# A four-layer image kernel: exponentials of one block on another engine, and statistics and copies in other places

## The chip, the cores and the metric

The kernel runs on one core of a Trainium2 chip. A core has engines that run side by side, each with its own queue of instructions: TensorE (PE in the profile; its weight loads are listed as PEld), which multiplies matrices into the accumulator memory PSUM; VectorE (DVE), which works elementwise; ScalarE (ACT), which evaluates functions such as the exponential; GpSimd (POOL); and SyncE (SP), which here only issues transfers (DMA) to and from the memory outside the core. Working data lies in the on-chip memory SBUF, 128 partitions wide. The metric is the device time of one execution in microseconds (us); less is better.

## The reference

The input `x` has shape (2, 128, 64, 64): two images of 128 channels, fp32. Four layers follow one another, each of the form `x = x + L(gn(x))`, where `gn` is a group normalization with 32 groups of four channels:

```python
def _gn(v, G=32, eps=1e-5):
    ...
    m = jnp.mean(g, axis=(2, 3, 4), keepdims=True)
    s = jnp.var(g, axis=(2, 3, 4), keepdims=True)
    return ((g - m) / jnp.sqrt(s + eps)).reshape(v.shape)
```

Layer 0 is an attention of four heads with convolutions around it; the change does not touch it. Layer 1 is a mix of convolutions; the two that matter here are `t8 = _conv(x, w8, (4, 4), dilation=(2, 2), groups=c)`, a 5 x 5 filter on each channel alone (25 "taps"), and a product with a matrix for each of seven rows. Layer 2 multiplies in the frequency domain: `rfft2` of the image, a product with complex 32 x 32 matrices at each of 64 x 33 frequencies, combined as quaternions, and `irfft2`. Layer 3 is a softmax attention with eight heads of 16 channels over all 4096 positions:

```python
a = jnp.einsum('bhcq,bhck->bhqk', q, k) / jnp.sqrt(jnp.float32(C))
a = jax.nn.softmax(a, axis=-1)
o = jnp.einsum('bhqk,bhck->bhcq', a, v)
```

## The kernel before, in words

**Frame.** The image stays in SBUF as `X`, 128 channels by 2 images by 4096 positions; each layer adds its output onto `X`. A chunk is 512 positions (`CH`), eight to an image. The layers run one after the other: layer 0 until 1500 us of the profile, layer 1's main part from 1537 to 1795, layer 2 to 2117, layer 3 to 3990. Within a layer the helper `_in_order` keeps TensorE's, VectorE's, ScalarE's and GpSimd's instructions in the order in which the program writes them; nothing is reordered. Side work is written as Python generators, and where a `next(...)` (or `some(gen, n)`, n times `next`) stands in the main loop decides where its instructions stand in each queue. Transfers are issued by SyncE in the order in which the program and their data allow.

**Statistics.** `_stats_steps` (L1433) computes a group normalization's mean and 1/sigma of one image in eleven steps. Each of the first eight measures one chunk on VectorE (L1444); the ninth combines them (L1447); the tenth has one TensorE matmul that averages over a group (L1450), followed by three small VectorE operations; the eleventh has a second such matmul (L1462), and then a VectorE operation (L1429) and a power on GpSimd (L1430). A normalization is `scale * x + shift`, so a shift, minus the mean times the scale, is needed as well.

**Layer 1, main part.** For each image, eight chunks follow one another. For each, TensorE runs `combined` (L710, the rows' products, 14 matmul records in the profile) and, before chunks 0 and 2, `on_tiles` (L681, the first four taps as diagonal matrices; ScalarE copies them out, L691). VectorE then adds the previous chunk's result onto `X` (`added`, L721), and `some(rest, ...)` (L760) advances the second image's remaining taps, 2 to 4 VectorE operations of 2.4 us each (L662). After them `some(steps, 2)` (L761) takes two steps of the statistics of image 0, which layer 2 will use; the steps exist only while image 1 runs.

**Layer 2.** First `shifted` (L851) makes the shift of image 0 on VectorE; `normalized` (L860) makes the normalized image on ScalarE (L868), `columns` (L882) transposes it on TensorE with a VectorE copy (L888), and `transformed` does the first Fourier step. Then eight blocks `kb` of frequency rows follow. In each, `products` (L1002) multiplies the spectrum by the layer's weights in two runs, the "direct" rows and the "mirrored" rows; weights arrive by DMA. Beside a run of products, `alongside` advances a list of generators: `rows_in` (L983) transposes and transforms rows of the spectrum on TensorE and then copies them (`placed`, L946) into the operand `e`, permuted and signed as the quaternion product wants it. A row needs twelve copies, of which eight, those with `r` 1 and 3, are of 32 partitions by 136 elements. In each pair of rows the first row's copies go to ScalarE (L960) and the second's to VectorE (L962). Block 0 has no previous block's output to work on, so beside its direct products the side list (L1128) holds the copies for its own mirrored products: those of the first pair of rows, and transposition, transformation and copies of the second pair. At the layer's end each image is turned back in eight steps: `turned_back` (L1154) transposes on TensorE, ScalarE copies, `added` (L1169) transforms and VectorE adds onto `X`; the two are skewed by `_skewed`, so that one is a step ahead of the other. While image 1 is turned back, each step takes two steps (L1163) of image 0's statistics for layer 3.

**Layer 3.** The heads and images form four groups (image `b`, half `t`), each with eight query blocks of 512 positions, and for each block 32 key tiles of 128 positions. For each tile, `scores` (L2311) fills two accumulators of two banks each (L2316, four matmuls of the program); for each of the two, the exponential is taken by ScalarE in one operation (L2330, 128 x 1024) or, for the pairs in `BY_VECTOR` (L1332), by VectorE with a polynomial: `exponentials` (L2269) makes eight VectorE operations (L2272, L2277, L2280, four of L2288, L2292), advanced one step a tile. There are four such pairs a block, at tiles 5, 12, 20 and 27. Three tiles (`LAG`) after the scores `multiply` (L2332) adds the product of the exponentials with the values onto the block's accumulator (L2339); the tables `ORDER` (L1344) put the pairs computed by VectorE some six tiles, for the last one four tiles, later in that sum. Three score accumulators take six PSUM banks. The two banks left (`acc`) serve the block's running product, the projections of queries, keys and values, and the bound.

The first block of the first group is also where that group's operands are made. `queries_and_keys` (L2190) makes, for one chunk, a projection (L2197), two shuffles (L2200, L2202) and five more elementwise operations (on ScalarE for the first two chunks, otherwise VectorE: L2211 to L2216), sends the three results out by DMA (L2219, `stack`), and reduces their largest absolute values (L2223). `stacked` (L2233) brings them back in the layout that the scores need, query pieces `q` and key pieces `k`. `values` (L2238) makes the values of four tiles (L2243, and one VectorE addition, L2250). These generators are advanced by one step every second tile until they are done; after that the bound (`bound`, L2257: VectorE L2260 and L2262, a matmul L2264, VectorE L2266) is taken. The later groups' operands are made during the group before.

**Other names.** The tile `st` (L2536) holds means and scales for layers 0 to 3. Layer 1 gets a view `there` of it, in which it leaves the statistics of image 0 for layer 2, which gets the same view as `here`.

Of the kernel before, what the change touches and what calls it, by code (L numbers as in the profile page):

```python
# [10 lines left out]
F32 = mybir.dt.float32  # L11
AF = mybir.ActivationFunctionType
ALU = mybir.AluOpType
# [6 lines left out]
NCH = S // CH  # L20
# [511 lines left out]
def _layer1(ctx, tc, X, a, cst, here=None, there=None, consts=None):  # L532
# [190 lines left out]
    def some(gen, n):  # L723
        for _ in range(n):
            next(gen, None)
# [23 lines left out]
    for b in range(B):  # L749
        for c in range(NCH):  # L750
            if c in (0, 2):
                z = on_tiles(g[b], t2[b], c // 2)
            ps = combined(t9[b], t2[b], c)

            for x in ready:
                added(*x)
            ready = [(b, c * CH, ps)]
            if c in (1, 3):
                ready.append((b, c // 2 * S // 2, z))
            some(rest, (4, 2, 4, 2, 3, 2, 2, 2)[c])  # L760
            some(steps, 2)  # L761
        if there is not None and b == 0:
            for x in ready:
                added(*x)
            ready = []
            steps = _stats_steps(nc, two, bank, X[:, 0, :], cst, mhalf, there)
# [36 lines left out]
def _layer2(ctx, tc, X, weights, cst, src, here=None, there=None, beside=None):  # L803
# [26 lines left out]
    with tc.tile_pool(name="l2_a", reuse_waits="tile", bufs=3) as ap, tc.tile_pool(  # L830
# [23 lines left out]
        scales = [st]  # L854
        shifts = [shifted(st)]
        if B > 1:
# [53 lines left out]
    with tc.tile_pool(name="l2_e", reuse_waits="tile", bufs=4) as ep, tc.tile_pool(  # L910
# [34 lines left out]

        def placed(kb, m, got, image, e, scalar):  # L946

# [19 lines left out]
            copied(2, 1)  # L967
            yield
            for r in (1, 3):
                for p in range(4):  # L970
                    copied(r, p)
                yield
# [9 lines left out]

        def rows_in(kb, rows, places, es):  # L983

            yts = [transposed(m) for m in rows]
            yield
            gots = [transformed(m, yt) for m, yt in zip(rows, yts)]
            yield
            yield from copies(kb, rows, gots, places, es)

        def copies(kb, rows, gots, places, es):
            for image in places:
                if es[image] is None:
                    es[image] = ep.tile([128, 4, 2 * PAIRS, 8 * B], F32, tag="e", name="e")
                yield from together(
                    *(
                        placed(kb, m, got, image, es[image], i % 2 == 0)
                        for i, (m, got) in enumerate(zip(rows, gots))
                    )
                )  # L1000
# [114 lines left out]
        for kb in range(BLOCKS2):  # L1115
# [7 lines left out]
            if before:  # L1123
                side += [turned(pzs[1], before[1]), back(kb - 1, *before)]
                n += 6
            else:
                later = side
                side, n = [copies(0, first[:2], gots[:2], (1,), e), rows_in(0, first[2:], (1,), e)], 8  # L1128
            alongside(
# [18 lines left out]
    with tc.tile_pool(name="l2_c", reuse_waits="tile", bufs=3) as cp, tc.tile_pool(  # L1148
        name="l2_cps", reuse_waits="tile", bufs=4, space=PSUM
    ) as cps:  # L1150
        for b in range(B):
            xi = X[:, b, :].rearrange("p (h w) -> p h w", w=W)

            def turned_back(i):  # L1154
                pt = cps.tile([128, CH], F32, tag="pt", name="ps_pt")
                for n in range(4):
# [5 lines left out]
                    )  # L1162
                for _ in range(2):  # L1163
                    next(steps, None)
# [974 lines left out]
def _layer3(ctx, tc, X, l3, cst, out, worst, here, dram):  # L2139
# [158 lines left out]
    class Group:  # L2298

        def __init__(self, b, t, f, idle=0):  # L2300
            self.b, self.t, self.f, self.ac = b, t, f, None
            self.kept, self.q, self.k = {}, {}, {}
            self.vt = two.tile([128, NQT, 2, 3, 16], F32, tag="vt", name="vt")
# [7 lines left out]
    def scores(g, qb, kt):  # L2311
# [11 lines left out]
        for p in range(2):  # L2323
            g.weights[qb, kt, p] = w = []
            if (kt, p) in BY_VECTOR:
                chain[0] = exponentials(ps[p], w)
# [5 lines left out]
    def multiply(g, qb, at):  # L2332
        if at == 0:
            g.ac = acc()
        for j in range(4):

            i, kt = j % 2, ORDER[j // 2][at]
            (w,) = g.weights[qb, kt, j // 2]
# [188 lines left out]
def kernel(ctx, tc, a, out):  # L2527
# [4 lines left out]
    with tc.tile_pool(name="keep", bufs=1) as keep:  # L2532
        X, cst, eps5 = _inputs(tc, keep, a)

        worst = keep.tile([128, 1 + 2 * B], F32, name="worst")
        st = keep.tile([128, B + 2, 2], F32, name="st")  # L2536
        rows_of_weights = _layer0(tc, X, a, cst, worst, st[:, :B], dram)
# [86 lines left out]
```

## Time and profile before

| | |
|---|---|
| time, median of three runs | 4001.92 us (4000.72 to 4008.1) |
| profiled execution, its own time | 4003.18 us |
| its span, first to last instruction | 4001.4 us |
| TensorE busy | 3853.4 us (96%) |
| ScalarE busy | 3243.5 us (81%) |
| VectorE busy | 3200.6 us (80%) |
| GpSimd busy | 86.2 us (2%) |
| DMA | 217.59 MB, mean 54 GB/s |
| mean granted TensorE clock | 0.987 of full speed |

The page gives the busy time of each engine, the same by slices of the span, the chain of work that ended last, and groups of instructions with the idle time before them and what ended it. Shares of the whole span are averages over stages with different limits. By stage, the windows view gives (us):

| stage | length | PE | DVE | ACT |
|---|---|---|---|---|
| layer 1, main part, 1537 to 1795 | 258 | 244.09 | 237.79 | 72.39 |
| layer 2, 1795 to 2117 | 322 | 284.10 | 218.44 | 187.90 |
| layer 3, 2117 to 3990 | 1873 | 1857.37 | 1407.24 | 1785.63 |

Two groups of the page are those of layer 3's exponentials: L2330 on ScalarE, 1920 operations of 1062 ns, busy 1781.3 us; and on VectorE 128 sets of steps, for instance L2272, 128 operations of 1224 ns.

### The profile page before, as it was taken

The numbers are of one execution on the slowest core, as the hardware profiler recorded it, in microseconds if no ns is written. First come the engines' busy times: TensorE is split into PE (matmuls) and PEld (weight loads), VectorE is DVE, ScalarE is ACT, GpSimd is POOL, SyncE is SP. The second block draws the span as 40 slices with busy tenths as digits, with TensorE's granted clock in tenths as the row PEclk, the third lists the DMA queues.
The fourth block names the chain that finished last, engine by engine and source line by source line (L and its number), as shares of the span: only waits on it lengthen the run. The fifth ranks groups of instructions, "written<-read, shape, count | busy, mean of one in ns | idle before, by whom it ended". The sixth has DMA issues, their size and how long they took to land.

```text
span 4001.4 us, 82144 instructions
## 1 busy us (share of the span) xinstructions
PE 3853.4 (96%) x35202; PEld 1313.9 (33%) x35202; DVE 3200.6 (80%) x3577; ACT 3243.5 (81%) x3948; POOL 86.2 (2%) x145
## 2 busy tenths in 40 slices
PE   7999999989999998998998999999999999999998
PEld 4511221353111124446664232232233222322222
DVE  6599999858999998996758777777777777776666
ACT  4499999736899983226645999999999999999998
POOL 1000000000000001000000000000000000000000
PEclk9999999999999999999998999999999999999999
DMA  1199960000000000004744110110002000110000
GB/s 51 23 200 185 187 106 2 1 2 2 2 2 2 2 2 13 6 19 199 280 199 150 32 32 25 53 46 31 26 27 72 30 27 25 44 47 6 6 6 5
DMA packets 193128, 217.59 MB, mean 54 GB/s; under 512 B 30441, under 2 KB 154345, under 8 KB 188658
## 3 DMA queue, kind: packets, MB, share of 16 engines
q1 hardware_dynamic: 192754, 212.25, 20.5%
q8 instruction: 278, 4.55, 0.5%
q14 instruction: 96, 0.79, 0.1%
HBM read 178.64 MB, written 98.57 MB: 69 GB/s over the span
## 4 chain that ended last, share of the span: by engine, by line
PE 78%; DVE 10%; issue 4%; ACT 2%; POOL 0%; SPq 0%; DMA 0%; ACTq 0%; POOLq 0%; DVEq 0%
PE ps_acc L2339 25%; PE ps_s L2316 19%; PE ps L1884 11%; PE ps L1892 11%; DVE X L662 3%; PE ps_z L1024 2%; PE ps_bank L710 2%; DVE sums L1915 2%; PE ps L1645 2%; DVE e L962 1%; PE ps_bank L681 1%; PE ps_bank L1078 1%; PE ps_acc L2197 1%; PE ps_acc L2243 1%; PE ps_pe L937 1%
## 5 line engine op out<-in xcount | busy, mean ns | idle before, releaser
L2330 ACT ACTIVATE weights<-ps_s 128x1024 f32<-128x1024 f32 x1920 | 1781.3, 1062 | 75.6 <-PE ps_s L2316 75.4
L2339 PE MATMUL ps_acc<-weights,vt 128*32 128x512 f32 x8192 | 1092.9, 605 | 0.0
L1915 DVE TENSOR_TENSOR sums<-sums,weights 128x2048 f32<-128x2048 f32 x384 | 854.2, 2283 | 3.5 <-ACT weights L1967 1.4
L2316 PE MATMUL ps_s<-q,k 64*128 64x512 f32 x4096 | 830.3, 469 | 3.7 <-DMA k<-stack 2.4
L1967 ACT ACTIVATE weights<-ps 128x1536 f32<-128x1536 f32 x512 | 740.6, 1447 | 6.9 <-PE ps L1892 6.9
L2316 PEld LDWEIGHTS ps_s<-q,k 64*128 64x128 f32 x4096 | 348.3, 184 | 935.2 <-ACT weights L2330 808.8
L1892 PE MATMUL ps<-q,k 32*64 32x512 f32 x8192 | 574.0, 612 | 3.6 <-ACT weights L1964 3.0
L1884 PE MATMUL ps<-weights,vt 128*32 128x512 f32 x4096 | 544.7, 604 | 0.0
L2288 DVE SCALAR_TENSOR_TENSOR exp_z<-exp_z,exp_m 128x1024 f32<-128x1024 f32 x384 | 469.0, 1221 | 9.3
L1964 ACT ACTIVATE weights<-ps 128x512 f32<-128x512 f32 x512 | 306.8, 599 | 75.3 <-PE ps L1892 36.5
L2272 DVE TENSOR_SCALAR exp_i<-ps_s 128x1024 int32<-128x1024 f32 x128 | 156.7, 1224 | 216.7 <-PE ps_s L2316 216.5
L2339 PEld LDWEIGHTS ps_acc<-weights,vt 128*32 128x32 f32 x8192 | 161.9, 108 | 309.6 <-issue 308.8
L1892 PEld LDWEIGHTS ps<-q,k 32*64 32x64 f32 x8192 | 120.0, 129 | 432.2 <-ACT weights L1964 381.7
L1884 PEld LDWEIGHTS ps<-weights,vt 128*32 128x32 f32 x4096 | 84.2, 108 | 390.9 <-issue 378.5
L662 DVE SCALAR_TENSOR_TENSOR X<-g,w,X 128x2048 f32<-128x2048 f32 x84 | 197.4, 2351 | 2.6
L2292 DVE SCALAR_TENSOR_TENSOR weights<-exp_z,exp_i 128x1024 f32<-128x1024 f32 x128 | 156.8, 1225 | 15.5 <-ACT weights L2330 0.5
L1915 DVE TENSOR_TENSOR sums<-weights 128x2048 f32<-128x2048 f32 x64 | 145.8, 2288 | 28.7 <-ACT weights L1967 27.9
L1645 PE MATMUL ps<-pad,diag 32*32 32x512 f32 x4032 | 151.8, 614 | 8.7 <-DVE qk L1656 4.1
L2288 DVE SCALAR_TENSOR_TENSOR exp_z<-exp_m 128x1024 f32<-128x1024 f32 x128 | 155.9, 1218 | 0.0
L1024 PE MATMUL ps_z<-w_ri,e 128*32 128x128 f32 x2048 | 142.9, 408 | 12.5 <-DVE e L962 6.9
L1645 PEld LDWEIGHTS ps<-pad,diag 32*32 32x32 f32 x4032 | 86.1, 104 | 69.3 <-issue 21.1
L962 DVE TENSOR_SCALAR e<-ps_pe 32x136 f32<-32x136 f32 (+1 forms) x341 | 101.1, 297 | 4.8
(321 smaller groups left out, 2943.0 us busy)
## 6 DMA issues: line engine op xcount, KB each, us to landing
w_ri<-w_r SPq DMA_DIRECT2D x16, 2112.0 KB, 8.1
w_ri<-w_i SPq DMA_DIRECT2D x16, 2112.0 KB, 13.0
stack<-qs SPq DMA_DIRECT2D x64, 256.0 KB, 2.1
q<-stack SPq DMA_DIRECT2D x128, 128.0 KB, 2.5
k<-stack SPq DMA_DIRECT2D x128, 128.0 KB, 2.6
stack<-ks SPq DMA_DIRECT2D x32, 256.0 KB, 2.1
w_r<-in_L_conv_kr_w SPq DMA_DIRECT2D x15, 528.0 KB, 12.6
w_r<-in_L_conv_kr_x SPq DMA_DIRECT2D x15, 528.0 KB, 12.6
```

The costliest lines, as they stand in the source:

```text
L662: nc.vector.scalar_tensor_tensor(xi, g[:, i : i + H // 2, j : j + W], w8[:, s : s + 1], xi, ALU.mult, ALU.add)
L1024: nc.tensor.matmul(out.rearrange("p (n f o) -> p n f o", n=2, f=2), e[:, s, 2 * j : 2 * j + 2, :].rearrange("p f x -> p (f x)"), w.rearran ...
L1645: nc.tensor.matmul(ps[r // 2][to, r % 2, :].rearrange("p (h w) -> p h w", w=W), diag[rows, grp, t, :], pad[rows, y0 : y0 + ROWS, t % 3 : t ...
L1884: nc.tensor.matmul(out[rows, :], lhs(rows), w[:, j, :], start=first, stop=stop)
L1892: nc.tensor.matmul(bank[64 * h : 64 * h + 64, :], k1[rows, kt * 128 + 64 * h : kt * 128 + 64 * h + 64], q1[rows, qb * CH : (qb + 1) * CH], ...
L1915: nc.vector.tensor_add(parts[p].rearrange("p j c -> p (j c)"), t.rearrange("p j c -> p (j c)"), w.rearrange("p j c -> p (j c)"),)
L1964: nc.scalar.activation(held[n][:, 0, :], single, AF.Exp)
L1967: nc.scalar.activation(held[n][:, 1:, :], three, AF.Exp)
L2288: nc.vector.scalar_tensor_tensor(z, x, n, m, ALU.add, ALU.mult)
L2316: nc.tensor.matmul(ps[j // 2][:, j % 2, :], g.k[kt // 4][rows, j // 2, keys], g.q[qb][rows, j // 2, :], start=True, stop=True,)
L2330: nc.scalar.activation(w[0], ps[p], AF.Exp)
L2339: nc.tensor.matmul(g.ac[32 * j : 32 * j + 32, :], g.vt[:, kt, j // 2, i : i + 2, :].rearrange("p a d -> p (a d)"), w[:, i, :], start=(at = ...
```

## The change

It has four edits.

1. In layer 1's main loop the steps of the statistics come before the taps of the same chunk, not after them, and they are spread 2, 2, 2, 2, 1, 1, 1, 0 over the eight chunks instead of 2 each until they are used up. The shift of image 0 is made there too, by one VectorE operation at the last chunk of image 1, ahead of the last two taps. `st` gets a third column for it, and layer 2 takes it from there.
2. In layer 2's block 0 the eight copies with `r` 1 and 3 of the second row of the second pair, for the mirrored products, go to ScalarE instead of VectorE.
3. At layer 2's end the steps of the statistics are spread 2, 2, 2, 2, 1, 1, 1, 0 as well.
4. In the first block of the first group of layer 3 no pair is left to VectorE: ScalarE takes all 64 exponentials, and the products are added in the order of the tiles. The number of VectorE operations falls by 32, that of ScalarE's exponentials rises by 4. Which of SyncE's transfers comes first changes for the last two key chunks, where query pieces come ahead of key pieces.

```diff
             if c in (1, 3):
                 ready.append((b, c // 2 * S // 2, z))
+            some(steps, (2, 2, 2, 2, 1, 1, 1, 0)[c])
+            if there is not None and b == B - 1 and c == NCH - 1:
+                nc.vector.scalar_tensor_tensor(
+                    there[:, 2:3], there[:, 0:1], -1.0, there[:, 1:2], ALU.mult, ALU.mult
+                )
             some(rest, (4, 2, 4, 2, 3, 2, 2, 2)[c])
-            some(steps, 2)
...
         scales = [st]
-        shifts = [shifted(st)]
+        shifts = [shifted(st) if here is None else here[:, 2:3]]
...
-        def placed(kb, m, got, image, e, scalar):
+        def placed(kb, m, got, image, e, scalar, helped=False):
...
             copied(2, 1)
             yield
+            scalar = scalar or helped
             for r in (1, 3):
                 for p in range(4):
                     copied(r, p)
...
-                side, n = [copies(0, first[:2], gots[:2], (1,), e), rows_in(0, first[2:], (1,), e)], 8
+                side, n = [copies(0, first[:2], gots[:2], (1,), e), rows_in(0, first[2:], (1,), e, True)], 8
...
-                for _ in range(2):
+                for _ in range((2, 2, 2, 2, 1, 1, 1, 0)[i]):
                     next(steps, None)
...
         def __init__(self, b, t, f, idle=0):
             self.b, self.t, self.f, self.ac = b, t, f, None
+            self.busy = idle > 0
...
-            if (kt, p) in BY_VECTOR:
+            if (kt, p) in BY_VECTOR and not (g.busy and qb == 0):
...
-            i, kt = j % 2, ORDER[j // 2][at]
+            i, kt = j % 2, at if g.busy and qb == 0 else ORDER[j // 2][at]
...
-        st = keep.tile([128, B + 2, 2], F32, name="st")
+        st = keep.tile([128, B + 2, 3], F32, name="st")
```

`rows_in` and `copies` pass the new argument `helped` on to `placed`. `idle` is 2 for the first group alone, so `busy` is true for that group only.

More of the change, by code (lines that the diff above doesn't have):

```diff
@@ L981, in together, with rows_in @@
                 yield
-        def rows_in(kb, rows, places, es):
+        def rows_in(kb, rows, places, es, helped=False):
             yts = [transposed(m) for m in rows]
@@ L988, in rows_in, with copies @@
             yield
-            yield from copies(kb, rows, gots, places, es)
-        def copies(kb, rows, gots, places, es):
+            yield from copies(kb, rows, gots, places, es, helped)
+        def copies(kb, rows, gots, places, es, helped=False):
             for image in places:
@@ L996, in copies @@
                     *(
[L997 removed]
+                        placed(kb, m, got, image, es[image], i % 2 == 0, helped)
                         for i, (m, got) in enumerate(zip(rows, gots))
```

## The prediction

> **What bounds the kernel now.** I read the page first, then the chain of waits, then the windows by stage, then the timeline at the four places that the diff touches. TensorE is busy 96% of the span and carries 78% of the chain. The Trainium skill warns of that figure ("Perfetto Trace Analysis", Identifying the Most-Contended Engine: matmul busy time says little about the distance to the limit), so I looked for gaps instead. The windows view (columns: stage, its length, busy time of PE, PEld, DVE, ACT, POOL, clock, DMA share, GB/s) shows where layer 3 has them:
>
> ```profile
> 2134.00:2202.00 68.00, 60.05 (x360) 21.67 (x358) 59.11 (x96) 47.93 (x51) 0.00 (x0) 0.91 0.57 187
> 2202.00:2260.00 58.00, 58.00 (x401) 17.29 (x397) 43.09 (x53) 55.48 (x61) 0.00 (x0) 1.00 0.08 26
> ```
>
> After 2202 a block takes about 58 us with TensorE full and ScalarE at 96%. The first block is another regime: TensorE 88%, ScalarE 70%, VectorE 87% against 74% later. The timeline there (start, length, engine, line, what, in brackets the idle time before and its releaser):
>
> ```profile
> 2151.65 0.69 DVE L2280 TENSOR_SCALAR exp_i<-exp_i 128x1024 int32<-128x1024 int32 x1
> 2161.80 1.13 PE L2197 MATMUL ps_acc<-X,wqk 128*128 128x512 f32 x2 [0.67 <-DVE vt L2250]
> 2172.63 1.13 PE L2197 MATMUL ps_acc<-X,wqk 128*128 128x512 f32 x2 [1.37 <-DVE vt L2250]
> 2183.20 1.13 PE L2197 MATMUL ps_acc<-X,wqk 128*128 128x512 f32 x2 [1.75 <-DVE vt L2250]
> 2196.95 0.35 PE L2264 MATMUL ps_acc<-mm,head_sum 128*128 128x1 f32 x2 [2.85 <-DVE mm L2262]
> 2197.90 1.91 PE L2339 MATMUL ps_acc<-weights,vt 128*32 128x512 f32 x8
> ```
>
> TensorE waits on VectorE for a shared accumulator bank and for the bound; VectorE's line at 2151.65 is one step of the exponentials that stand among that work; after the longest wait the same eight product matmuls take 1.91 us instead of 1.06. The other places, from the timelines of the end of layer 1, of layer 2's first products and of layer 2's end:
>
> ```profile
> 1773.42 0.56 PE L1450 MATMUL ps_bank<-gn_mv,consts 128*128 128x1 f32 x2 [4.86 <-DVE gn_mv L1447]
> 1782.42 0.16 DVE L1429 TENSOR_SCALAR st<-ps_bank 128x1 f32<-128x1 f32 x1 [2.42 <-PE ps_bank L1462]
> 1795.65 3.60 ACT L868 ACTIVATE g<-X,shift,st 128x512 f32<-128x512 f32 x3 [36.10 <-DVE shift L851]
> ```
>
> ```profile
> 1851.86 1.22 DVE L962 TENSOR_SCALAR e<-ps_pe 32x136 f32<-32x136 f32 x4
> 1853.18 0.67 PE L1024 MATMUL ps_z<-w_ri,e 128*32 128x128 f32 x8 [3.31 <-issue]
> ```
>
> ```profile
> 2110.39 0.35 PE L1450 MATMUL ps_stat<-gn_mv,consts 128*128 128x1 f32 x2 [2.47 <-DVE gn_mv L1447]
> ```
>
> The 3.31 us is labelled issue, but TensorE resumes 0.10 us after VectorE's last image copy, so I read it as that.
>
> **What the skill says.** "TensorE: Matmul & The Clock Gate", Part 1: an idle window of about 3.4 us halves the array's clock, until about as long a busy one. The trace agrees: after the 4.86 us wait, the matmuls of line 710 start 0.85 us apart, later 0.43. The same page (Architectural detail) calls VectorE's and ScalarE's queues strict FIFOs. That agrees: in the first block the adds of line 2250 stand behind the exponential's steps.
>
> **Part 1, statistics and shift in layer 1.** Same work, other places. Today at chunk 4 of image 1 TensorE's aggregate matmul stands behind three taps (7.13 us). The aggregate now goes before them and its matmul after chunk 5's products. Following VectorE from 1765.87, where nothing differs yet: aggregate 0.3, three taps 7.1 (1773.3), add 0.7 (1774.0). TensorE no longer waits at 1768.56; chunk 5 takes 6.1 us at the fast clock (1734.78 to 1741.4 shows 15 in 6.6), and the matmul ends at 1775.0. VectorE waits 1.0 there, then small steps 0.6, two taps 4.75, add 0.7 (1781.0); wait 0.6 for the second matmul, which follows chunk 6 (1781.1); two taps, add, shift 0.17, two taps, add: 1792.6. Today that add ends at 1795.38. ScalarE's first normalization can start before, once the shift is ready at 1787; but the first copy of transposes (line 888) stands on VectorE behind the last add and four statistics, 2.46 us, so the stage starts 2.8 us sooner, not 8. Ends: 2.0 and 3.3. Cover: TensorE finishes at 1787.6, 5 us ahead of VectorE.
>
> **Part 2, image copies.** For block 0's second pair of rows, eight 32x136 copies go from VectorE (about 0.31 us each, start to start) to ScalarE (0.29). ScalarE starts its copies at 1843.84; 20 end at 0.38 + 19 x 0.29 = 5.9 us later, 1849.8. TensorE's previous products end at 1849.88. So the mirrored products start at about 1850.0 instead of 1853.18: 3.2 us. With no pause the next transposes and transforms should run at the fast clock: after today's pause they take 1.12 and 1.99 us, elsewhere 0.71 and 1.09, hence up to 1.3 more; I take 0.9, together 4.1. Ends: 3.0 and 4.6. ScalarE's next work today starts at 1854.57, so the 2.3 us added is covered. The next weights, issued at 1849.91, take 12.8 us to land (1863); needed at 1869.
>
> **Part 3, statistics at layer 2's end.** The aggregate stays at 2109.88, since VectorE is busy until then, but its matmul goes one step later; TensorE does one more product and transpose before it, 1.33 us (the steady step there). Gain 1.3; ends 0.5 and 1.5. Layer 3 starts when VectorE has the last add, so it moves along.
>
> **Part 4, first block of layer 3.** VectorE loses four exponentials, eight steps each: 1.22 + 2 x 0.69 + 4 x 1.22 + 1.23, about 8.7 us of steps each, 34.8 us in all (its tail runs into block 2). ScalarE gains four of 0.94 us, 3.8 us. The bound's matmul keeps its place on TensorE, but its inputs are no longer queued behind steps. The SP queue has the same transfers; for the last two key chunks the query pieces go ahead of the keys.
>
> How fast can it go? Key tiles 8 to 11 in today's trace are all by ScalarE and have full key and value work: scores at 2153.37, 2155.03, 2157.75, 2159.41, and the next would be at 2162.13 but for the VectorE wait (the product matmuls end one period of 1.66 after 2159.41, plus 1.06 of keys). So 8.76 us a group of four. From tile 4 at 2143.91 (unchanged): tile 8 at 2152.7, 12 at 2161.4, 16 at 2170.2, 20 at 2178.9, against 2153.37, 2162.86, 2173.69 and 2184.26 today. From there ScalarE binds: its tile-22 pair starts at 2183.9 and the twenty exponentials up to tile 32 take 20 x 0.922 to 0.943 us (19 take 17.52 in a row after 2204.31; four take 3.77): tile 32 at 2202.6. Today 2204.31 + 8 x 0.922 = 2211.7. Gain 9.1; ends 5 and 10. Three score buffers keep TensorE to that pace, so nothing is hidden behind it. Keys arrive: chunk 4's last load lands 14.3 us after its projection; chunk 7's would at 2192.2, and tile 28 wants it at 2194.5.
>
> Later blocks are unchanged, 58 us each, and the offset is carried to the end.
>
> **Sum.** 2.8 + 4.1 + 1.3 + 9.1 = 17.3 us. The profiled execution took 4003.18 us, 1.8 more than its span, so it would become 3985.9; the median, 4001.92, lies 1.3 below the profiled time, so I forecast 3984.6.
>
> **Rivals.**
> *Keys late.* If loads land some 2 us later than I work out, each group waits for its keys and only 3 of part 4 remains: total 11.2, 3990.7. For it: a margin near 2 us at tile 28. Against: no wait on keys after the third tile today. Chance 0.12.
> *Early gains hidden.* Layer 2's start or end is paced by something else (buffers of the previous stage, a cold array), so parts 1 and 3 vanish: 13.2, 3988.7. For it: ScalarE is nearly full from 1801 on. Against: its first copy there waits for TensorE, which waits for VectorE. 0.13.
> *ScalarE binds the first block.* With every exponential its own it never catches up after the projections, so part 4 gives nothing: 8.2, 3993.7, no measurable change. Against: 7.54 us of 8.76 in the group of tiles 8 to 11. 0.05.
> *Slower: the granted clock.* Layer 3 takes 1870 us with TensorE full. If a denser start made the throttle grant 1.4% less over it, that is 26 us more, and 4010.8 in all; it decides from 0.93%. Against: 1.00 granted in blocks that are already full. 0.03.
> Main forecast 0.67, within 3981 to 3988.
>
> **Range and chances.** What a measurement can tell from no change is about 0.2%, 8 us. The main case and the first two rivals are beyond it: 0.92 faster; 0.05 same; 0.03 slower. The sum of low ends, 10.5, gives 3991.4; of high ends, 19.4, 3982.5, and the three runs of before scatter by some us: 3979.5 to 3991.5, which leaves out the last two rivals.
>
> **What would show it.** In the first block the waits of line 2197 on values and of the bound's matmul on VectorE gone, tile 32's first exponential some 23.7 us after tile 20's scores instead of 27.4, ScalarE unbroken from tile 22; line 1450's waits below 1 us in both places; no 3.31 us before the mirrored products. I am wrong if waits on keys, or on score buffers before tile 24, take their place, if VectorE's last add in layer 1 stays near 1795, or if layer 3's later blocks change length.

## The result, and the profile after

The changed kernel took 3992.23 us (median of seven runs, 3987.2 to 3994.9); seven runs of the kernel before, made together with them or shown above, have a median of 4008.1 us. The ratio is 0.9966, with a 95% interval of 0.9957 to 0.9976: 13.6 us less, between 9.6 and 17.2 (the two medians lie 15.9 us apart). The forecast was 3984.6 us, 17.3 us less, in a range up to 3991.5. So the direction held, the gain was smaller than forecast, and the time lies 0.7 us above the range. The profiled execution has a span of 3987.9 us where the one before had 4001.4.

The windows view of the changed kernel, over the first block of layer 3 and the second (columns: stage, its length, busy time of PE, PEld, DVE, ACT, POOL, granted clock, DMA share, GB/s):

```profile
2128.00:2188.30 60.30, 58.92 (x372) 21.96 (x372) 35.76 (x77) 50.88 (x55) 0.00 (x0) 0.92 0.67 218
2188.30:2246.00 57.70, 57.70 (x394) 17.25 (x386) 34.84 (x45) 55.88 (x61) 0.00 (x0) 1.00 0.09 27
```

The first block now nearly has the length of the later ones. TensorE is busy 98% of it (88% before), VectorE 59% (87%), ScalarE 84% (70%). TensorE's timeline in that block (start, length, engine, line, what):

```profile
2155.37 1.13 PE L2202 MATMUL ps_acc<-X,wqk 128*128 128x512 f32 x2
2164.12 1.12 PE L2202 MATMUL ps_acc<-X,wqk 128*128 128x512 f32 x2
2172.88 1.12 PE L2202 MATMUL ps_acc<-X,wqk 128*128 128x512 f32 x2
2183.28 0.38 PE L2269 MATMUL ps_acc<-mm,head_sum 128*128 128x1 f32 x2
2184.25 1.07 PE L2345 MATMUL ps_acc<-weights,vt 128*32 128x512 f32 x8
```

These are the lines that carried brackets before (2197, 2264 and 2339, now 2202, 2269 and 2345). The brackets are gone: the projections follow at 8.75 us, a group of four tiles; the bound's matmul waits for nothing, and the products behind it take 1.07 us, not 1.91.

The timelines of the other places: the end of layer 1, the copies of layer 2's block 0, and layer 2's end.

```profile
1777.72 0.28 PE L1455 MATMUL ps_bank<-gn_mv,consts 128*128 128x1 f32 x2
1784.34 0.16 DVE L1434 TENSOR_SCALAR st<-ps_bank 128x1 f32<-128x1 f32 x1 [0.32 <-PE ps_bank L1467]
1789.97 3.67 ACT L872 ACTIVATE g<-X,st 128x512 f32<-128x512 f32 x3 [27.20 <-DVE st L762]
1794.75 0.69 DVE L721 TENSOR_TENSOR X<-ps_bank,X 128x512 f32<-128x512 f32 x1
```

```profile
1844.69 2.04 ACT L964 ACTIVATE e<-ps_pe 64x136 f32<-64x136 f32 x7
1846.89 0.32 DVE L966 TENSOR_SCALAR e<-ps_pe,signs 128x136 f32<-128x136 f32 x1
1847.22 0.92 DVE L966 TENSOR_SCALAR e<-ps_pe 64x136 f32<-64x136 f32 x3
1848.23 3.49 ACT L964 ACTIVATE e<-ps_pe 32x136 f32<-32x136 f32 x12 [1.50 <-DVE e L966]
1851.78 0.64 PE L1029 MATMUL ps_z<-w_ri,e 128*32 128x128 f32 x8 [1.42 <-ACT e L964]
```

```profile
2107.74 0.35 PE L1455 MATMUL ps_stat<-gn_mv,consts 128*128 128x1 f32 x2 [1.14 <-DVE gn_mv L1452]
```

At layer 1's end the wait of 4.86 us is gone and that of 2.42 us is 0.32. At layer 2's end the wait fell from 2.47 to 1.14 us, by 1.33. At the copies something is left: TensorE still waits 1.42 us, and ahead of it ScalarE idles 1.50 us for VectorE's first copies of the same row.

### Where the time went, stage by stage

Both kernels have the same 35,202 matmul records in nearly the same order, so the start of one and the same record in two traces, each counted from its span's start, tells how far one is ahead. The table gives, for stretches between such records (named by their time in the trace of before), how much longer (+) or shorter (-) each run's trace was than the trace of before, in us. The first three stretches are layers 0 and 1 ahead of any edit, layer 1's end, and layer 2's start with the copies; "once more" is a third trace of the changed kernel.

| run | to 1735 | 1735 to 1810 | 1810 to 1873 | 1873 to 1900 | 1900 to 2100 | 2100 to 2118 | tiles 4 to 32 |
|---|---|---|---|---|---|---|---|
| changed kernel | +3.2 | -2.8 | -2.7 | -0.3 | -0.1 | -1.3 | -9.4 |
| again | -2.9 | -3.3 | -2.2 | +2.8 | +1.8 | -1.3 | -8.7 |
| once more | -1.0 | -3.3 | -2.2 | +2.9 | -1.5 | -1.3 | -9.4 |
| without the block | +1.3 | -2.8 | -2.7 | -0.3 | +5.7 | -1.3 | 0.0 |
| steps beside | -1.2 | -3.3 | -2.1 | +2.9 | -1.6 | -1.3 | +2.1 |
| last two back | -0.1 | -3.3 | -2.2 | +2.8 | -1.0 | -1.3 | -6.8 |
| last one back | -1.7 | -3.3 | -2.2 | +3.2 | +1.6 | -1.3 | -9.9 |
| block alone | -0.1 | -0.2 | 0.0 | -0.1 | -0.7 | 0.0 | -9.3 |
| layer 1 alone | +3.0 | -2.7 | +0.1 | +0.4 | 0.0 | 0.0 | 0.0 |
| copies alone | +0.2 | +0.5 | -2.2 | -0.3 | -0.3 | 0.0 | 0.0 |
| third column | -0.9 | -0.2 | 0.0 | -0.2 | -0.5 | 0.0 | 0.0 |

Each edit gives its gain where it stands, in every run that has it. What the forecast didn't have is in two places: the copies give 2.1 to 2.7 us and not 4.1; and between 1873 and 2100, where nothing was edited, three of the seven runs with the edits of layers 1 and 2 give back 4.6 to 5.4 us, three others 1.3 to 1.8. The changed kernel's first trace gives nothing back there; it lost 3.2 us ahead of the edits.

### The profile page after: what moved, and what is told of

Same layout as the page of the kernel before. It is cut to its first block, busy times and chain, and to the rows that moved or that the text cites. A ratio compares the mean times of both kernels' runs of the same rounds, so it can differ in the third digit from the quotient of the medians.

```text
span 3987.9 us, 82135 instructions
## 1 busy us (share of the span) xinstructions
PE 3850.2 (97%) x35202; PEld 1312.0 (33%) x35202; DVE 3164.6 (79%) x3537; ACT 3247.9 (81%) x3960; POOL 88.2 (2%) x145
## 4 chain that ended last, share of the span: by engine, by line
PE 83%; DVE 6%; issue 3%; ACT 3%; POOL 0%; DMA 0%; SPq 0%; POOLq 0%; ACTq 0%; DVEq 0%
PE ps_acc L2345 26%; PE ps_s L2322 19%; PE ps L1889 12%; PE ps L1897 11%; PE ps_bank L710 2%; PE ps_z L1029 2%; DVE sums L1920 2%; PE ps L1650 1%; PE ps_t L640 1%; DVE e L966 1%; PE ps_bank L590 1%; PE ps_bank L681 1%; PE ps_bank L1083 1%; PE ps_acc L2248 1%; PE ps_acc L2202 1%
## 5 line engine op out<-in xcount | busy, mean ns | idle before, releaser
L2293 DVE SCALAR_TENSOR_TENSOR exp_z<-exp_z,exp_m 128x1024 f32<-128x1024 f32 x372 | 454.4, 1222 | 9.1
L2368 DVE STREAM_TRANSPOSE z<-ps_acc 128x512 f32<-128x512 f32 x32 | 22.9, 717 | 103.1 <-PE ps_acc L2345 103.1
## 6 DMA issues: line engine op xcount, KB each, us to landing
w_ri<-w_i SPq DMA_DIRECT2D x16, 2112.0 KB, 13.2
```

The costliest lines, as they stand in the source:

```text
L2293: nc.vector.scalar_tensor_tensor(z, x, n, m, ALU.add, ALU.mult)
```

## The experiments

All ratios are to the kernel before, run on the same chip. The median of before was 4001.8 to 4004.4 us in the later runs.

### Is the loss part of the change? Layout, repetition, parts

The first run has the wider tile alone:

```diff
-        st = keep.tile([128, B + 2, 2], F32, name="st")
+        st = keep.tile([128, B + 2, 3], F32, name="st")
```

> The kernel before, with the tile st three columns wide and the third never used: no instruction is added or moved, only addresses in SBUF. Chance theory (the 3.2 us that the changed kernel's trace loses in layer 0 and at layer 1's start, ahead of the first edit, are where the clock's windows happened to fall): ratio 1.0000 within 0.001, and TensorE's matmuls before 1735 us stand anywhere within some 3 us of the profile before. Layout theory (the wider tile costs the 3.2 us): ratio 1.0008, and layer 1's chunks stand 3.2 us later than in the profile before.

Measured: 1.0002 (0.9994 to 1.0011); 0.9 us less than before up to 1735. The wider tile costs nothing. Over the runs, the stretch ahead of any edit varies by 6 us, up to 2.3 of them at layer 1's start, where the records show anything from 10 to 17 us at half the granted clock.

The changed kernel itself, a second time:

> The changed kernel once more. Chance theory: ratio 0.9957 (17.4 us of about 4006, the sum of the four places in the traces), since the losses outside them are no part of the change. If the losses belong to the change (layout, or layer 3's later blocks growing by 0.9 us): 0.9966 again, and the trace shows 3 us lost before 1735 again and the same drift of 0.9 us between 2240 and 3700.

Measured: 3989.02 us, 0.9964 (0.9952 to 0.9976). Neither theory of the two: 2.9 us were gained ahead of 1735 this time, not lost, and still the ratio is 0.9964. The trace shows why: +2.8 and +1.8 us between 1873 and 2100, where the first trace had lost nothing. So a loss does belong to the change, but not the one that I had named. The drift in layer 3's later blocks, 0.9 us in the first trace, is 0.6 us in this one.

Two runs split the change. The first takes only the edits of `Group`, `scores` and `multiply` from the diff, the second all the others.

> Only the edit of layer 3's first block. Parts-add theory: from tile 4 to tile 32 of the first block 57.2 us instead of 66.55, 9.4 us, ratio 0.9977 (0.9974 if the shorter run-in of tiles 0 to 4, 0.7 us, comes along). Theory that it only works with the earlier edits: less than 5 us, 0.9988 or above.

Measured: 0.9978 (0.9969 to 0.9987); tiles 4 to 32 take 57.26 us (66.56 before). The 9.3 us come without the earlier edits.

> The changed kernel without the edit of layer 3's first block. Parts-add and chance: 2.8 + 2.9 + 1.3 = 7.0 us, ratio 0.9983, with tiles 4 to 32 taking the 66.5 us of before. Layout theory: 7.0 - 3.2 = 3.8 us, 0.9991. Early gains hidden (the first rival of the forecast on them): layer 3's start less than 3 us earlier, ratio 0.9993 or above.

Measured: 0.9991 (0.9984 to 0.9997), so 3.6 us and not 7.0; tiles 4 to 32 take 66.52 us. The table shows the three edits giving 6.8 us at their places, and +5.7 us between 1900 and 2100 in that trace. "Early gains hidden" is nearly right by the sum and wrong by the place: they arrive, and are lost later. The layout theory's 0.9991 is met by chance, since the wider tile costs nothing. This traced execution (4003.18 us) is 5 us slower than the run's median, so its 5.7 us are not what the run loses as a rule.

The edit of layer 1 and that of the copies, each alone:

> Only the edit of layer 1 (statistics ahead of the taps, the shift made there). Places theory: between TensorE's chunk products at 1735 us and layer 2's transposes at 1810 us the kernel gains 2.7 us, ratio 0.9993. Clock theory of what is left over: in layer 2 after 1872 us the stretches at half the granted clock lie elsewhere than before, because the stage starts at another point of the 3.41 us grid, and their sum between 1800 and 2110 us changes by several windows either way (30.7 us before, 44 to 48 us in two of the runs with the edits of layers 1 and 2). If instead an earlier start itself brings more half-clock windows, the run has over 40 us of them and ratio 1.0000 or more.

> Only the edit of layer 2's copies. Places theory: the mirrored products of block 0 come 1.8 to 1.9 us sooner and by 1872 us the gain is 2.7 us, ratio 0.9993. Clock theory as in the run of layer 1 alone. If the gain is lost to something the copies push aside (ScalarE's next work, or weights that land no sooner), it is gone again by 1900 us, in the same place in this run as in all others with the edit.

Measured: 0.9994 (0.9986 to 1.0002) and 0.9993 (0.9985 to 1.0002). The gains at the places are 2.7 and 2.2 us, and alone neither edit loses more than 0.5 us after 1873. Between 1873 and 1900 both traces have 6.8 us at half the clock, as has that of before. In the second trace of the changed kernel it is 13.7 us.

### The first block: VectorE's queue or the order of the products?

Here VectorE computes the four exponentials as well, into a tile that nobody reads:

```diff
                 nc.scalar.activation(w[0], ps[p], AF.Exp)
+                if (kt, p) in BY_VECTOR:
+                    chain[0] = exponentials(ps[p], w, False)
+                    next(chain[0])
```

> The changed kernel, and in layer 3's first block VectorE runs the eight steps of the four exponentials all the same, with a result that nobody reads; ScalarE takes all 64 as well. VectorE-queue theory (the first block was held by values, keys and the bound standing behind those steps): tiles 4 to 32 take 66 us or more again instead of 57.2, and TensorE's waits on VectorE's value additions return; ratio 0.9989 or above. Order theory (what helps is that no product waits for a VectorE exponential and that the sums run in the order of the tiles): 57.2 us stays, ratio 0.9965.

Measured: 0.9988 (0.998 to 0.9997); tiles 4 to 32 take 68.68 us. TensorE's waits in the first block of this run (the waits view: who waited for whom, us in total, times, longest):

```profile
PE ps_acc L2202 <- DVE vt L2255: 3.7, 3, 1.7
PE ps_s L2324 <- DMA k<-stack: 2.8, 1, 2.8
PE ps_acc L2269 <- DVE mm L2267: 2.3, 1, 2.3
```

The waits on values and on the bound are those of before, and the keys' transfer (tile 0's) is in both kernels. The order of the products is the changed one and ScalarE still takes all 64 exponentials, so neither is what helped; the steps on VectorE's queue were the cause.

How much of VectorE's share can come back? Once the pairs at tiles 20 and 27, once that at 27 alone:

```diff
+LATE = {(20, 1): 26, (27, 1): 31}
+FIRST = [_order(p, LATE) for p in range(2)]
...
-            if (kt, p) in BY_VECTOR and not (g.busy and qb == 0):
+            if (kt, p) in (LATE if g.busy and qb == 0 else BY_VECTOR):
```

> The changed kernel, but in the first block the pairs at tiles 20 and 27 go back to VectorE. In the changed kernel ScalarE sets the pace of tiles 27 to 39 (1.83 us each instead of 1.66). ScalarE theory: two exponentials less give 1.9 us, tile 40 34.8 us after tile 20 instead of 36.65; ratio 0.9960. VectorE-queue theory: the steps from tile 20 on stand ahead of the last keys and of the bound, and TensorE's wait for the bound returns at tile 24 with up to 2.8 us; net between 1 us of loss and 1 us of gain, ratio 0.9965.

> The changed kernel, but in the first block the pair at tile 27 alone goes back to VectorE. VectorE-queue theory: at tile 27 keys, values and the bound are done, so no wait returns (the bound's matmul at tile 24 stays below 0.5 us), and ScalarE, which paces tiles 27 to 39, has one exponential less: tile 40 comes 35.7 us after tile 20 instead of 36.65. If any exponential of VectorE's in this block costs, the bound's wait or a later one returns with 1 us or more. Ratio 0.9962.

Measured: with two back, tile 40 comes 39.15 us after tile 20 (36.65 in the changed kernel), ratio 0.9972 (0.9962 to 0.9982), and TensorE waits again:

```profile
PE ps_acc L2271 <- DVE mm L2269: 2.6, 1, 2.6
```

With one back it is 36.07 us, without a wait; ratio 0.9969 (0.9959 to 0.9979). The line lies between tiles 20 and 27. The pair at tile 20 stands ahead of the bound and costs some 3 us, more than the 1 us that I had set as the limit for both; the pair at tile 27 comes after it and gains 0.6 us, a little less than the 0.95 us expected.

### The copies: a wait between the engines

The forecast let ScalarE make its 20 copies in a row. The run lets it make those of the first row before the ones taken over, so that VectorE's first copies of the second row are done by then:

```diff
             yield
+            if helped and not scalar:
+                yield
             scalar = scalar or helped
```

> The changed kernel; in block 0 ScalarE makes all copies of the pair's first row before the eight that it took over, one turn later than in the change. Cross-wait theory (the eight stand behind VectorE's first copies of the same row, for which ScalarE idles 1.50 us in the changed kernel): the idle falls below 0.4 us and TensorE's pause before the mirrored products from 1.42 us to 0.2 to 0.4 us. If the copies themselves bind (20 of 0.29 us), the pause stays at 1.4 us. Ratio 0.9961 against 0.9964, which the timing can't tell apart; the trace decides. Clock theory for what follows: TensorE loses 2.8 us between 1872 and 1900 us, or nothing, by where the stage stands on the 3.41 us grid.

Measured, from the timeline at the copies:

```profile
1843.13 2.33 ACT L964 ACTIVATE e<-ps_pe 32x136 f32<-32x136 f32 x8 [0.34 <-DVE e L966]
1845.51 0.64 PE L1031 MATMUL ps_z<-w_ri,e 128*32 128x128 f32 x8 [0.27 <-ACT e L964]
```

TensorE's pause fell from 1.42 to 0.27 us: the copies waited, they did not bind. The stretch 1810 to 1873 is 3.8 us shorter than before, against 2.2 to 2.7. The time (0.9966, 0.9954 to 0.9978) doesn't tell it from the changed kernel.

### Layer 3's start, and three edits together

The next run keeps TensorE busy through two waits at layer 3's start:

```diff
+    def warm(n):
+        ps = spp.tile([128, 2, CH], F32, tag="sp", name="ps_warm")
+        for _ in range(n):
+            nc.tensor.matmul(ps[:, 0, :], head_sum, X[:, 0, :CH], start=True, stop=True)
...
+            if g.busy and n == 0:
+                warm(3)
             scores(g, qb, kt)
...
         next(keys)
+        if c == 1:
+            warm(3)
         next(g.values)
```

> The changed kernel, with six more matmuls on TensorE at layer 3's start, whose results nobody reads: three before the values of chunk 1, where TensorE waits 3.6 us, and three before the first scores, where it waits for keys. Clock theory: the 17 us at half the granted clock that follow layer 3's start vanish or halve, tiles 0 to 4 take 8.7 us instead of 9.9, and the gain of 1.2 us is carried to the end, ratio 0.9961. Rival: the first tiles wait for the keys' transfers and for ScalarE whatever the clock, tiles 0 to 4 stay at 9.9 us, or the added matmuls delay tile 0 by up to 2 us.

Measured: 0.9972 (0.9962 to 0.9983). The time at half the clock after layer 3's start fell from 17.1 to 3.4 us, and tiles 0 to 4 took 8.73 us instead of 9.9. But from layer 3's first matmul to tile 0 it took 0.5 us longer, so 0.7 us of the 1.2 expected is left, and this execution lost 6.2 us between 1900 and 2100. Of little worth by itself.

> The changed kernel with the three edits together: copies in turn, the pair at tile 27 back on VectorE, TensorE kept busy at layer 3's start. If they add: 1.2 + 0.9 + 1.2 = 3.3 us below the changed kernel, ratio 0.9956. If the clock's windows decide what layer 2 keeps, the sum shows in the trace at the three places and the total lies anywhere within some 4 us of it.

Measured: 3986.75 us, 0.9958 (0.9945 to 0.9972). Two of the three gains show at their places: 3.8 us between 1810 and 1873, and 9.9 us in tiles 4 to 32. The third does not: 6.8 us at half the clock are left after layer 3's start, and tiles 0 to 4 take 9.76 us. The total lies below the changed kernel's, but the intervals overlap.

### What takes back the gain in layer 2

Six of layer 2's eight blocks have a pause of 0.8 us on TensorE between the inverse transforms of the two images; the second waits for ScalarE's copy of the first. The granted clock in the records changes on a grid of 3.41 us. In the second trace of the changed kernel, one such pause lies inside one window of the grid and one across an edge (TensorE's timeline, then the windows view on the grid):

```profile
1883.29 0.94 PE L1083 MATMUL ps_bank<-consts,pzt 66*128 66x128 f32 x6 [0.81 <-ACT y L1086]
...
1946.42 1.83 PE L1083 MATMUL ps_bank<-consts,pzt 66*128 66x128 f32 x14 [0.81 <-ACT y L1086]
```

```profile
1880.99:1884.40 3.41, 2.60 (x24) 2.41 (x23) 2.81 (x6) 0.72 (x1) 0.00 (x0) 1.00 0.85 277
1884.40:1891.23 6.83, 6.83 (x53) 5.09 (x55) 0.73 (x3) 3.08 (x9) 0.00 (x0) 0.50 1.01 430
1942.43:1945.85 3.42, 3.18 (x34) 2.31 (x32) 3.29 (x10) 0.99 (x3) 0.00 (x0) 1.00 0.45 99
1945.85:1949.26 3.41, 2.84 (x26) 2.31 (x26) 1.13 (x2) 1.24 (x2) 0.00 (x0) 1.00 0.93 401
1949.26:1952.67 3.41, 3.41 (x44) 2.37 (x47) 1.13 (x4) 2.26 (x8) 0.00 (x0) 1.00 1.01 431
```

After the first, two windows follow at clock 0.50; after the second none. I counted this over the fourteen traces taken up to then: of 55 such pauses that lie whole in a window, 49 are followed by half the clock in the next one, and the other six touch an edge of the window within 0.06 us; of 29 that an edge splits, none is. Where the pauses lie depends on when layer 2 runs against the grid, and the edits shift it by 2 to 5 us. Between 1873 and 1900, seven of the ten executions with both edits lost 2.6 to 3.2 us to it, and none of the five without.

These pauses are not the whole loss between 1900 and 2100. At layer 2's end every one of the twenty traces has a pause of 1.8 us ahead of a matmul of line 1058. In four it is followed at once by 10.2 to 13.7 us at half the clock, in which 3.5 to 5.5 us are lost: 4.0 of the 5.7 us of the run without the block, 5.5 of the 6.2 us of the run that keeps TensorE busy. Here too the place on the grid seems to decide, but otherwise than above: in these four the pause begins at most 0.6 us ahead of an edge or 0.5 us behind one, in the other sixteen 0.59 to 2.26 us behind one. No run tested this.

Two runs tried to take those pauses away by letting the side list run two steps ahead beside the direct products (first in the changed kernel, then in the kernel before):

```diff
-                n += 6
+                n += 8
```

> The changed kernel; in layer 2's blocks the side list advances by two more steps beside the direct products, so that four products stand between the two images' inverse transforms on TensorE (0.35 us of work where TensorE today waits 0.8 us for ScalarE's copy). Window theory (a pause of 0.8 us that lies whole inside one 3.41 us window brings half the clock in the next, which is what ate part of the gain of layers 1 and 2): the pauses fall to 0.45 us, most half-clock windows between 1880 and 2050 us vanish (from 20 us or more to under 10 us), and the kernel gains 3 to 6 us over the changed one: ratio 0.9950 to 0.9957. Rival (the half-clock windows follow from the load, wherever the pauses lie): their number stays, ratio 0.9963.

> The kernel before with that same edit alone. Window theory: 2 to 5 us less than before, ratio 0.9988 to 0.9995, since its phase splits two of six pauses already and four windows go. Rival: 1.0000.

Measured: 0.9965 (0.9952 to 0.9979) and 1.0011 (1.0003 to 1.002). The pauses of 0.8 us are gone, but in each block another of some 3 us stands before a product (TensorE's waits of the first of the two runs, from 1872 to 2060):

```profile
PE ps_z L1029 <- DMA w_ri<-w_i: 10.2, 3, 4.0
PE ps_z L1029 <- DVE z L1038: 8.8, 3, 3.0
```

Three of the six are put down to weights that land late, three to VectorE. The first of these weights are issued at 1886.4 us, against 1880.6 in the second trace of the changed kernel; that the products end later and hold the weights' buffers longer is a reading that no run tested. Both ratios are nearer to the rival's 0.9963 and 1.0000 than to the window theory's, and the first run still has 20.5 us at half the clock between 1880 and 2050, where under 10 were expected. With new pauses in the place of the old ones, these runs could not settle it. At one place they speak for the windows: the first of them reached 1873 at the same point of the grid as five others that lost 2.8 to 3.2 us up to 1900, and lost nothing there. A sixth, the run with the copies in turn, stood there too and lost 0.3 us, so this is a hint and no more.

One more execution of the changed kernel tests the rule on a trace that had not been used to find it:

> The changed kernel once more, one look. Window theory: which of its six pauses in layer 2 lie whole inside a window of the 3.41 us grid tells which are followed by half the clock, as in the runs so far (no pause that a window's edge splits is followed by one); the layer's length between 1872 and 2100 us follows from that count. Rival: no such rule holds in a new execution.

Measured (3987.24 us, a single execution): four pauses whole in a window, all four followed by half the clock; two split, none followed. It lost 2.9 us between 1873 and 1900.

> The changed kernel with all four edits: copies in turn, the pair at tile 27 back on VectorE, TensorE kept busy at layer 3's start, inverse transforms apart. If they add: 3 us from the first three and 3 to 6 us from the last, ratio 0.9942 to 0.9950, below both kernels clear of the interval of the changed one's 0.9966. If the windows only move elsewhere: 0.9957.

Measured: 3981.99 us, 0.9952 (0.9938 to 0.9965), between the two expectations.

The last two runs remove the pause without moving an instruction. The second image's transform takes a PSUM bank of the other kind:

```diff
-                pq = bank()
+                pq = bank("pe" if b else "bank")
```

> The changed kernel; in layer 2's blocks the second image's inverse transform uses a PSUM bank of the other kind, which is free by then, so that TensorE need not wait 0.8 us for ScalarE's copy of the first image. No instruction moves on any engine. Window theory: the 0.8 us pauses go (at most 0.3 us left), and with them the half-clock windows that follow them: between 1880 and 2050 us at most 7 us at half the clock instead of 14 to 27; gain over the changed kernel 5 us from the pauses themselves (six or seven of 0.8 us) and 3 to 8 us from the clock: ratio 0.9933 to 0.9945. Rival (the load, not the pauses): the clock falls elsewhere as often, and at most the 5 us come, ratio 0.9952; if the bank isn't free in time, 0.9964.

> That edit together with copies in turn, the pair at tile 27 back on VectorE and TensorE kept busy at layer 3's start. If they add: another 3 us, ratio 0.9925 to 0.9938. If the windows only move elsewhere: as the run of the bank alone.

Measured: 3973.21 us, 0.992 (0.9907 to 0.9934); with the other three edits 3972.91 us, 0.9917 (0.9904 to 0.9931). TensorE's waits between 1872 and 2060, in the second trace of the changed kernel (two upper lines) and with the other bank:

```profile
PE ps_z L1029 <- DVE e L966: 5.3, 6, 0.9
PE ps_bank L1083 <- ACT y L1086: 4.8, 6, 0.8
```

```profile
PE ps_z L1029 <- DVE e L966: 5.3, 6, 0.9
PE ps_bank L1058 <- DVE pz L1046: 3.0, 2, 1.6
```

Line 1083's wait is gone as a whole, the longer ones of line 1029 stay as they were. Line 1058's waits belong to the layer's end, which this run reaches sooner. The windows view over the same blocks, in the same two runs:

```profile
1880.00:2050.00 170.00, 160.25 (x1899) 109.43 (x1888) 122.83 (x337) 104.81 (x318) 0.00 (x0) 0.92 0.71 282
```

```profile
1880.00:2050.00 170.00, 163.13 (x2069) 107.54 (x2070) 132.27 (x360) 108.71 (x327) 0.00 (x0) 0.99 0.78 307
```

The granted clock rises from 0.92 to 0.99, and 2069 matmul records fit where 1899 did. Between 1873 and 2100 this trace is 12.9 us shorter than that of before: 4.8 us are the six pauses, and the other 8 us fit the clock: 10.2 us at half of it instead of 27.3. Against the second trace of the changed kernel, which has 37.5 us at half the clock there, the stretch is 17.5 us shorter. Between 1873 and 1900 it loses nothing, though the first pause would have lain whole in a window: the second transform starts at 1884.53, 1.2 us behind an edge of the grid. So the half-clock windows after these pauses follow from them. By the ratios the other bank takes some 18 us off the changed kernel, more than the 8 to 13 expected and more than the change took off the kernel before; the three small edits beside it add nothing that can be measured.

## Why the prediction was right or wrong

**What bounds the first block (part 4): right.** Forecast was 8.76 us for a group of four tiles, 35.0 from tile 4 to 20; measured 35.01. From tile 20's scores to tile 32's first exponential it said 23.7 us, measured 23.07: ScalarE runs unbroken from tile 22, as forecast, at 0.90 us an exponential instead of the 0.922 to 0.943 used. From tile 4's scores to tile 32's the block takes 57.16 us for 66.56, 9.4 us less, where 9.1 was forecast. That VectorE's queue was the cause is shown by the run that put the steps back. "Keys late" and "ScalarE binds" are ruled out: no wait on keys after tile 0, and 7.5 us of ScalarE in a group of 8.75.

**Part 1: right.** 2.8 us forecast; 2.7 to 3.3 measured in twelve traces and 2.1 in three more, and the stage did start with VectorE's last add, not with the shift that was ready at 1790.

**Part 2: the mechanism right, the sum mis-sized.** The step that failed is "20 end at 0.38 + 19 x 0.29 = 5.9 us later". It priced ScalarE's queue and no wait in it. The eight copies stand behind VectorE's first copies of the same row, and those behind a VectorE transpose: 1.50 us. The pause fell from 3.31 to 1.42 us, not to nothing; with the warm clock 2.1 to 2.7 us for the 4.1 forecast. The run with the copies in turn shows that wait and removes it.

**Part 3: right.** 1.3 us forecast, 1.33 in every trace with the edit.

**The sum: the step that failed is "2.8 + 4.1 + 1.3 + 9.1 = 17.3 us", with nothing for a loss in the stretches between the edits.** At their places the four parts give some 16 us: part 2 is 1.4 to 2.0 us short. The rest fits the clock, which was carried as if layer 2 ran alike wherever it started. In seven of ten executions 2.6 to 3.2 us are lost between 1873 and 1900, and between 1900 and 2100 the same executions range from 1.6 us gained to 6.2 lost. Which of these the seven executions of the result had is not known: only one of them has a trace, and it lost nothing there. The forecast named a cold array only as a thing that might pace the start of layer 2 or its end, in the rival "early gains hidden"; that rival's sum, 13.2 us, is what came, but by luck and not by its way. The forecast's rule of the clock, an idle window of about 3.4 us, left no room for what pauses of 0.8 us do; already in the trace of before the clock fell 2.7 us into the wait of 4.86 us (idle from 1768.56, half the clock from 1771.31), so that trace didn't bear the rule out. I had also used the clock's effect as a gain (0.9 us in part 2) and never as a loss, though the trace of before had half-clock windows all through layer 2.

**The level.** The three runs of before had a median of 4001.92; the seven of the result have 4008.1, and the later runs 4001.8 to 4004.4. The forecast leaned on three runs that spread over 7.4 us. Its range took 3 us off the sum of high ends for that scatter and added nothing at the other end: 3991.5 is the sum of low ends, 3991.4, although one of the three runs lay 6 us above their median. With the same ratio on the first median the time would have been 4001.92 x 0.9966 = 3988.3, within the range but far from its middle; the missing 3 to 4 us of gain are the error, and the level put it outside.

**The granted clock as the slower rival: not seen.** It was sought in layer 3's full blocks, where the changed trace has 1.00 as before. The clock acted in layer 2, with a few us.

## What to carry to other kernels

When an engine's work goes to another engine, follow not only the two queues but the waits between them: copies into one tile can stand behind the first engine's copies even where the new owner is free. An engine that is busy 87% in one stage can bound it through a single shared bank: taking 34.8 us of steps off its queue there gave 9.3 us here. A short pause on TensorE can have a price beyond its length where the clock falls after it: look for pauses that repeat in every block, and try another buffer for them before shaving work elsewhere.

## What the runs showed of the hardware

The granted clock of TensorE changes in the records on a grid of 3.41 us, and stretches at half of it are whole multiples of that. A single pause of 0.8 us can be enough: those before line 1083 were followed by half the clock in 53 of 59 cases where they lay whole in a window of the grid, with the execution that tested it, and in none of 31 where an edge split them. That is much less than the idle window of about 3.4 us that the prediction worked with; the measurement decides. The clock then costs more than the pause itself: in the run without these pauses 17 us less at half the clock between 1873 and 2100 than in the changed kernel's first trace, and some 8 us gained from it beside the 4.8 us of the six pauses.

What exactly the clock goes by stays open. It isn't the busy time in a window: a window at 76% (1880.99 above) was followed by half the clock, and in the same trace one at 46% was not, with a pause of 1.84 us:

```profile
2078.97:2082.38 3.41, 1.57 (x20) 0.87 (x12) 2.81 (x11) 0.36 (x1) 0.00 (x0) 1.00 0.00 0
2082.38:2085.80 3.42, 3.19 (x29) 3.15 (x29) 0.00 (x0) 1.47 (x4) 0.00 (x0) 1.00 0.00 0
```

Nor is it the length of the pause: those of 0.9 us before line 1029, whole in a window, were followed by half the clock in 9 of 57 cases only between 1880 and 2050 in those fourteen traces, and in 18 of 69 with the last such pause, near 2053, counted too. The pause of 1.8 us at line 1058 was followed at once in 4 of 20. And a stretch of full work can stand at half the clock for long; in the last run TensorE was busy throughout one of 10 us at layer 2's end, which follows that pause of 1.8 us:

```profile
2068.00:2078.30 10.30, 10.30 (x50) 9.91 (x49) 0.00 (x0) 2.82 (x7) 0.00 (x0) 0.50 0.00 0
```
